# A planned one-core transformer block: quantization's powers of two copied by ScalarE, one buffer for MLP and quantization, other stage offsets

## The chip, the cores and the metric

The kernel runs on one core of a Trainium2 chip. Its engines are TensorE (PE, with weight loads listed apart as PEld), VectorE (DVE), ScalarE (ACT), GpSimd (POOL) and SyncE (SP), which here issues every DMA. Matrix products land in PSUM; all else lies in SBUF or in DRAM. Each engine takes its instructions in the order of its own list and waits for semaphores of the others.

The metric is the device time of one execution in microseconds, lower is better. Before the change it is 7728.81 us, the median of 3 runs (7723.64 to 7744.94).

## The reference

The input x has 16 sequences of 1024 tokens with 256 channels, all in fp32. Four residual steps follow each other:

```
x = x + attention(layernorm(x))     # 16 heads of 16, rotary, causal; Wqkv, Wproj
x = x + ffn(layernorm(x))
x = x + mixer(layernorm(x))         # returns y + silu(rmsnorm(y) @ w1.T) @ w2.T, y = z + mamba(rmsnorm(z))
x = x + ffn(layernorm(x))
```

The mamba part is an input product, a convolution over 4 tokens, a recurrence over 1024 steps for 512 channels with 16 states each, a gate and an output product. The step that the change is about is ffn. It takes blocks of 32 channels, divides each by its greatest absolute value over 7.5, rounds to the nearest value of a grid of six bits (ties to the lower one), multiplies back, and multiplies by a weight that was quantized in the same way:

```
scales = max(max|block| / 7.5, 1e-30)
q = nearest_on_grid(block / scales)     # grid: m/8 below 1, (1 + m/8) * 2^(e-1) above
out = (q * scales) @ (wq * ws).T + bias
```

## The kernel before

**Tiling and stages.** Each sequence is cut into two halves of 512 tokens, which gives 32 half sequences m; f = m % 2 tells the first half from the second. Work on one m is written as eight stages, each a function: `stage_a` (0: layernorm, transposes, queries and keys, rotary), `stage_m` (1: the scores' row maxima, for 8 pairs of heads), `stage_e` (2: values, scores again, exponentials, the product with the values), `stage_p` (3: output product, residual, and the first ffn), `stage_b` (4: mamba's inputs), `stage_s` (5: the recurrence, by VectorE's scan), `stage_o` (6: mamba's output product, rmsnorm), `stage_c` (7: the MLP, residual, and the second ffn). Stages p, b, o and c work on two tiles of 256 tokens, one after the other (i0 = 0 and 2). Stage c runs the MLP for each 128 tokens: for two groups of four hidden tiles a group of w1 products into a ps tile, a tanh by ScalarE and a multiply by VectorE into a hid tile, and then one group of 8 x w2 products from both hid tiles.

**Order.** Nothing is issued when a stage is called. `Graph` records each instruction (or group) as a node with its dependencies and an estimated cost (`add`, L971, and `_cost`, L1232). `prepare` (L1014) gives each node a due time: its place in its stage, counted by cost and spread over 32 units, one per half sequence, plus the stage's entry in OFFSETS. SP's nodes are due LEAD earlier, and nodes of other engines that read a ps tile URGENT earlier. `run` (L1058) then plays the program with the estimated costs: whenever an engine is free, it takes the ready node with the lowest due time whose tiles can be had. `emit` writes the instructions in that order, all from line 1167, so the profile tells groups apart by tile names and not by lines. The list of each engine is thus fixed before the kernel runs; what takes longer on the chip than in the plan makes an engine wait at the head of its list.

**Tiles.** A tile is taken from a ring of buffers when its first node is placed, and freed when its last user is done. Four rules bear on what follows:

- PSUM has six `ps` tiles of 128 x 512, shared by all stages, and one `av` and one `y`. `AT_ONCE` limits how many ps tiles a stage may hold. Within a stage ps tiles are taken in program order (`turn`, L1052 to L1056, tested in `lacks`, L1076); hid tiles likewise.
- The node that takes a ps tile also takes at once the tiles that its later users would take (L1036 to L1044), so that a product does not lie in PSUM with no place to go.
- Two nodes of different engines on the same PSUM tile are always ordered, reads too (L996).
- `y_s`, stage e's result, has two buffers, and one half sequence fills both (one for each 128 channels). Stage p's transposes of i0 = 0 and of i0 = 2 read both.

**The quantization** (`quantize`, L230 to L260) is called from `feed_forward` (L271), in stage p and in stage c, for both i0, and once for the weight: 129 times. VectorE finds the blocks' maxima; GpSimd multiplies the source by the inverse into r, which lies in the destination tile. VectorE masks the exponent bits into e (a ps tile), raises it to at least 1, and writes the exponent of the inverse into t (a hid tile). GpSimd multiplies r by t. ScalarE adds two constants in turn, which rounds: into odd (a ps tile) and into r. VectorE takes the smaller of the two into r, then takes off the constant and multiplies by e into t. GpSimd multiplies t by the scale into the destination. `feed_forward` then transposes the result into another hid tile (hT) and multiplies it by the weight.

The change touches `hid_tile` (L227), `quantize`, `feed_forward` (L276), `stage_c` (L801 to L825), and the numbers in BUFS, OFFSETS, LEAD, AT_ONCE and URGENT (L845 to L853).

Of the kernel before, what the change touches and what calls it, by code (L numbers as in the profile page):

```python
# [13 lines left out]
I32 = mybir.dt.int32  # L14
AF = mybir.ActivationFunctionType
ALU = mybir.AluOpType
# [3 lines left out]
P = 128  # L20
NT = T // P
KC = C // P
NH, DH = 16, 16
HT = T // 2
# [8 lines left out]
EXP_BITS = 0x7F800000  # L33
# [3 lines left out]
MAGIC = 1.5 * 2.0**21  # L37
# [3 lines left out]
def block_kernel(ctx: ExitStack, tc: tile.TileContext, a, out: bass.AP):  # L41
# [10 lines left out]
    g = Graph(raw, pools)  # L52
    nc = g

    def ps_tile():
        return g.tile([P, 512], "ps", 6, "psum", as_needed=True)
# [5 lines left out]
    def t2_tile(tag):  # L62

        return g.tile([P, 2, C], tag, BUFS[tag])
# [63 lines left out]
    vaug = wp.tile([P, BUFS["vaug"], VPAD], F32, tag="vaug", name="vaug")  # L128
# [8 lines left out]
    for n, tag in ((HT, "qt"), (HT, "kt"), (HT // 2, "dk"), (HT, "sh")):  # L137
        made = []
        for i in range(BUFS[tag]):
            t = wp.tile([P, n], F32R, tag=f"{tag}{i}", name=f"{tag}{i}")  # L140
# [6 lines left out]
    for i in range(BUFS["ovz"]):  # L147
        t = wp.tile([P, 512], F32, tag=f"ovz{i}", name=f"ovz{i}")
# [10 lines left out]
    def small(shape, tag, name):  # L159

        return g.tile(shape, f"{tag}_{name}", 2)
# [9 lines left out]
    def layernorm(x, dst, name):  # L171

        n = x.shape[1]
        st = small([P, n, 6], "st", name)
        mv = small([P, n, 2], "mv", name)
        with g.group():
            for i in range(n):
                nc.vector.bn_stats(out=st[:, i, :], in_=x[:, i, :])
                nc.vector.bn_aggr(out=mv[:, i, :], in_=st[:, i, :])
        rs = rstd_of(mv[:, :, 1], n, LN_EPS, name)  # L180
        shift = small([P, n], "sh", name)
        with g.group():
            nc.gpsimd.tensor_scalar_mul(shift, mv[:, :, 0], -1.0)
            nc.gpsimd.tensor_tensor(out=shift, in0=shift, in1=rs, op=ALU.mult)
        for i in range(n):
            nc.scalar.activation(
                dst[:, i, :], x[:, i, :], AF.Identity, bias=shift[:, i : i + 1], scale=rs[:, i : i + 1]
            )
        return mv[:, :, 1], rs
# [11 lines left out]
    def transpose_into(dst, src):  # L201

        ps = ps_tile().rearrange("p (c t) -> p c t", c=KC)
        with g.group():
            for c in range(KC):
                for i in range(2):
                    nc.tensor.transpose(ps[:, c, i * P : (i + 1) * P], src[:, i, c * P : (c + 1) * P], ident)
        nc.scalar.copy(dst, ps)

    def linear(dst, lhs, nk, w, biased=False):  # L210

        ps = ps_tile().rearrange("p (t c) -> p t c", c=C)
        with g.group():
            for i in range(2):
                for k in range(nk):
                    nc.tensor.matmul(
                        ps[:, i, :],
                        lhsT=lhs[k][:, i * P : (i + 1) * P],
                        rhs=w[:, k, :],
                        start=(k == 0),  # L220
                        stop=(k == nk - 1 and not biased),
                    )
                if biased:
                    nc.tensor.matmul(ps[:, i, :], lhsT=ones, rhs=bias, start=False, stop=True)
        nc.vector.tensor_tensor(out=dst, in0=dst, in1=ps, op=ALU.add)

    def hid_tile():  # L227
        return g.tile([P, HT], "hid", BUFS["hid"], as_needed=True)

    def quantize(src, dst, name):  # L230

        nb = 2 * C // 32
        shp = [P, nb, 32]
        srcb, dstb = (v.rearrange("p t (k e) -> p (t k) e", e=32) for v in (src, dst))
        amax = small([P, nb], "amax", name)
        inv = small([P, nb], "inv", name)
        most = ps_tile()[:, 0:nb]
        nc.vector.tensor_reduce(out=most, in_=srcb, axis=AX.X, op=ALU.max, apply_absolute_value=True)
        nc.vector.tensor_scalar(amax, most, 1.0 / 7.5, 1e-30, ALU.mult, ALU.max)
        nc.vector.reciprocal(out=inv, in_=amax)  # L240
        nc.scalar.mul(amax, amax, 0.5)
        t = hid_tile().rearrange("p (k e) -> p k e", e=32)
        r = dstb
        nc.gpsimd.tensor_tensor(
            out=r, in0=srcb, in1=inv.unsqueeze(2).to_broadcast(shp), op=ALU.mult
        )

        e = ps_tile().rearrange("p (k e) -> p k e", e=32)
        nc.vector.tensor_single_scalar(e.bitcast(I32), r.bitcast(I32), EXP_BITS, ALU.bitwise_and)
        nc.vector.tensor_single_scalar(e, e, 1.0, ALU.max)  # L250
        nc.vector.tensor_single_scalar(t.bitcast(I32), e.bitcast(I32), EXP_BITS, ALU.bitwise_xor)
        nc.gpsimd.tensor_tensor(out=r, in0=r, in1=t, op=ALU.mult)
        odd = ps_tile().rearrange("p (k e) -> p k e", e=32)
        for i, v in enumerate((odd, r)):
            nc.scalar.activation(v, r, AF.Identity, bias=magic[:, i : i + 1])
        nc.vector.scalar_tensor_tensor(r, r, -0.25, odd, ALU.add, ALU.min)
        nc.vector.scalar_tensor_tensor(t, r, -MAGIC, e, ALU.add, ALU.mult)
        nc.gpsimd.tensor_tensor(
            out=dstb, in0=t, in1=amax.unsqueeze(2).to_broadcast(shp), op=ALU.mult
        )  # L260
# [10 lines left out]
    def feed_forward(x, name, tag):  # L271

        h = t2_tile(tag)
        layernorm(x, h, f"f{name}")
        quantize(h, h, name)
        hT = hid_tile().rearrange("p (c t) -> p c t", c=KC)  # L276
        transpose_into(hT, h)
        linear(x, [hT[:, c] for c in range(KC)], KC, wd, biased=True)

# [515 lines left out]
    def stage_c(m):  # L795
        r2T = shifted.pop(m)
        for i0 in range(0, HNT, 2):
            x = t2_tile("c2")
            nc.sync.dma_start(out=x, in_=vds[m][i0 // 2])
            for i in range(2):  # L800
                hids = []  # L801
                t0 = (i0 + i) * P
                for k0 in range(0, NF, 4):
                    ps = ps_tile().rearrange("p (f t) -> p f t", f=4)
                    with g.group():
                        for k in range(4):
                            for c in range(KC):
                                nc.tensor.matmul(
                                    ps[:, k, :],
                                    lhsT=w1[:, c, (k0 + k) * P : (k0 + k + 1) * P],  # L810
                                    rhs=r2T[:, c, t0 : t0 + P],
                                    start=(c == 0),
                                    stop=(c == KC - 1),
                                )
                    psf = ps.rearrange("p f t -> p (f t)")
                    hidf = hid_tile()
                    hids.append(hidf)
                    nc.scalar.activation(hidf, psf, AF.Tanh, scale=0.5)
                    nc.vector.scalar_tensor_tensor(hidf, hidf, 1.0, psf, ALU.add, ALU.mult)
                ps = ps_tile()[:, 0:C]  # L820
                with g.group():
                    for k in range(NF):
                        nc.tensor.matmul(
                            ps,
                            lhsT=hids[k // 4][:, k % 4 * P : (k % 4 + 1) * P],  # L825
                            rhs=w2[:, k, :],
                            start=(k == 0),
                            stop=(k == NF - 1),
                        )
                nc.vector.tensor_tensor(out=x[:, i, :], in0=x[:, i, :], in1=ps, op=ALU.add)  # L830
            feed_forward(x, "b", "c2")
            nc.sync.dma_start(out=tokens(out, m, i0), in_=x)


    stages = (stage_a, stage_m, stage_e, stage_p, stage_b, stage_s, stage_o, stage_c)
    for m in range(2 * B):
        for s, stage in enumerate(stages):
            g.stage = s
            stage(m)
    g.prepare(OFFSETS, LEAD, URGENT)  # L840
    order = g.run()
# [1 line left out]


BUFS = {"kt": 4, "qt": 2, "dk": 3, "sh": 2, "ovz": 3, "ov": 2, "pt": 2, "hb": 4, "dx": 5, "a2": 1, "p2": 2, "y_s": 2, "b2": 2,  # L845
        "o2": 2, "c2": 2, "rot": 3, "hid": 2, "vaug": 8, "carry": 40}
W4 = 3

OFFSETS = (0.0, -0.3, -0.5, 0.2, 2.3, 4.1, 4.5, 5.3)
LEAD = 0.3  # L850

AT_ONCE = {("ps", 1): 4, ("ps", 2): 4, ("ps", 3): 3, ("ps", 5): 2}
URGENT = 0.1  # L853

# [87 lines left out]
class Graph:  # L944
# [113 lines left out]
    def run(self):  # L1058
# [17 lines left out]
        def lacks(n):  # L1076
            wanted = {}
            for t in n.reserve:
# [3 lines left out]
                wanted[s] = wanted.get(s, 0) + 1  # L1082
                full = s.held.get(t.line, 0) + wanted[s] > AT_ONCE.get((s.name, t.line), 99)
                if full or len(s.free) < wanted[s] or t.turn >= s.taken.get(t.line, 0) + wanted[s]:
# [285 lines left out]
```

## Time and profile before

| | |
|---|---|
| median of 3 runs | 7728.81 us |
| the profiled execution's own time | 7733.1 us |
| its span, first to last instruction | 7731.2 us |
| mean granted TensorE clock | 0.915 |
| DMA | 1460.35 MB, 62.2% of 16 engines' time |
| POOL idle before hb<-dx,bc | 953.1 us, of it 712.1 on PE's y and 169.1 on loads of dx |
| hid's MLP activations / copies of hT | 256 / 128 |

Where the stages of one half sequence lie in time is read from the starts of instructions that each stage alone has. For m = 16:

| stage | mark | us from the span's start |
|---|---|---|
| e | first and last write of y_s | 3631 to 3764 |
| p | last multiply of its two quantizations | 3790 and 3838 |
| b | first copy of rT, last store of dd | 3825 and 4006 |
| s | first multiply into hb, last gate yg | 4101 to 4373 |
| o | copies of r2T | 4396 and 4435 |
| c | last multiply of its two quantizations | 4524 and 4640 |

From stage s of m = 1 to that of m = 30 a half sequence takes 231 us. The last write of y_s (m = 31) is at 7283, 448 us before the end.

How to read the profile: a row gives line, engine, operation, output<-inputs with buffer numbers left out, shapes and count, then busy time and the mean of one in ns, then the engine's idle time before them and what ended most of it. Tiles that come from `t2_tile` carry the first letter of their tag (p in stage p, c in stage c), `ps` is any of the six PSUM tiles, w any of mamba's work tiles. A wait is named by what came last. Share of busy time is an average over 32 half sequences with a start and an end, so the windows view, which gives busy times for chosen stretches, stands beside the page.

### The profile page before, as it was taken

Reading aid. Unit: us, or ns where it says so; the run is one execution under the profiler, and the core shown is the slowest. Engines: PE = TensorE matmul, PEld = TensorE weight load, DVE = VectorE, ACT = ScalarE, POOL = GpSimd, SP = SyncE. Lnnn points to the kernel's source line nnn. Section 1 sums busy time; section 2 is a strip of 40 time slices with the busy share of each in tenths; the row PEclk is TensorE's granted clock in tenths of the full one; section 3 lists DMA queues with packets and bytes.
Section 4 is the critical chain, followed back from the end, with each engine's and each line's share of the span. In section 5 each row is a group of like instructions: output and inputs, shape, how many; then the busy total and the mean of one; then the engine's idle time right before and its main releaser. Section 6 shows DMA issues by size and latency. Waiting matters only on the chain. (4 is left out here: it accounts for less than half of the span.)

```text
span 7731.2 us, 133194 instructions
## 1 busy us (share of the span) xinstructions
PE 7019.5 (91%) x43012; PEld 4061.3 (53%) x43012; DVE 6308.6 (82%) x12351; ACT 5308.7 (69%) x11348; POOL 5016.3 (65%) x3948
## 2 busy tenths in 40 slices
PE   6999999999999999999999899999999999999866
PEld 4444555555455555555555555555555555555434
DVE  3488988888887878888888788888988888888885
ACT  3667677776767667676776767777676776867652
POOL 2366757665676666676666676666767766665784
PEclk8988999999999898998999899999999999999877
DMA  4566766765676566665656666566766666665562
GB/s 148 164 194 215 206 194 192 210 189 173 206 210 196 170 187 201 193 212 168 208 177 198 196 193 211 176 204 195 209 198 195 208 181 194 212 192 168 160 180 70
DMA packets 978300, 1460.35 MB, mean 189 GB/s; under 512 B 92720, under 2 KB 410800, under 8 KB 977600
## 3 DMA queue, kind: packets, MB, share of 16 engines
q1 hardware_dynamic: 977600, 1451.84, 62.2%
q8 instruction: 339, 5.55, 0.3%
q14 instruction: 361, 2.96, 0.1%
HBM read 1044.63 MB, written 371.20 MB: 183 GB/s over the span
## 5 line engine op out<-in xcount | busy, mean ns | idle before, releaser
L1167 POOL TENSOR_TENSOR hb<-dx,bc 128x1024 f32<-128x1024 f32 x1024 | 2411.8, 2365 | 953.1 <-PE y L1167 712.1
L1167 ACT ACTIVATE pt<-ps 128x512 f32<-128x512 f32 (+1 forms) x2560 | 1258.5, 557 | 499.0 <-PE ps L1167 478.9
L1167 ACT ACTIVATE ps<-dx,amat 128x512 f32<-128x512 f32 x2048 | 1402.2, 700 | 132.8 <-DVE hb L1167 95.2
L1167 DVE TENSOR_TENSOR_SCAN ps<-ps,h_carry,hb 128x512 f32<-128x512 f32 x768 | 963.4, 1278 | 121.8 <-ACT ps L1167 71.7
L1167 DVE TENSOR_TENSOR hb<-ps,ct 128x512 f32<-128x512 f32 x1536 | 1022.6, 680 | 8.1
L1167 DVE TENSOR_TENSOR_SCAN ps<-ps,hb 128x512 f32<-128x512 f32 x768 | 922.9, 1218 | 96.3 <-ACT ps L1167 40.9
L1167 PE MATMUL av<-pt,vaug 128*32 128x512 f32 (+3 forms) x6144 | 934.3, 536 | 36.3 <-ACT pt L1167 31.0
L1167 PE MATMUL ps<-qt,kt 64*128 64x512 f32 (+3 forms) x3072 | 799.0, 457 | 101.4 <-ACT pt L1167 20.8
L1167 POOL TENSOR_TENSOR hb<-hb,ct 128x1024 f32<-128x1024 f32 x256 | 604.9, 2363 | 340.4 <-ACT h_carry L1167 186.2
L1167 PE MATMUL y<-hb,ysel 128*32 128x512 f32 x4096 | 670.1, 655 | 84.4 <-POOL hb L1167 37.3
L1167 PEld LDWEIGHTS ps<-qt,kt 64*128 64x128 f32 x3072 | 349.5, 194 | 609.7 <-issue 148.8
L1167 PE MATMUL ps<-sh,ones 64*128 64x512 f32 (+3 forms) x3072 | 630.8, 370 | 5.4 <-DMA sh<-mr 5.2
L1167 POOL TENSOR_TENSOR w<-w,w 128x1024 f32<-128x1024 f32 x192 | 454.5, 2367 | 145.3 <-ACT w L1167 121.6
L1167 PE MATMUL ps<-r2T,w 128*128 128x128 f32 x4096 | 529.5, 285 | 15.5 <-ACT pt L1167 4.3
L1167 PEld LDWEIGHTS ps<-r2T,w 128*128 128x128 f32 x4096 | 492.1, 197 | 78.9 <-issue 22.3
L1167 PEld LDWEIGHTS ps<-kt,qt 64*128 64x128 f32 x3584 | 324.7, 205 | 388.0 <-issue 132.5
L1167 PE MATMUL ps<-kt,qt 64*128 64x128 f32 (+1 forms) x3584 | 460.4, 324 | 54.7 <-ACT pt L1167 14.1
L1167 PE MATMUL ps<-rT,w 128*128 128x512 f32 x1024 | 500.6, 616 | 9.2 <-ACT ovz L1167 1.9
L1167 ACT ACTIVATE ovz<-ps 128x384 f32<-128x384 f32 (+2 forms) x1024 | 366.2, 412 | 200.9 <-PE ps L1167 192.1
L1167 PE MATMUL ps<-dk,qt 64*128 64x256 f32 (+1 forms) x2560 | 405.4, 348 | 102.8 <-DVE mx L1167 24.7
L1167 PE MATMUL ps<-w,hid 128*128 128x256 f32 x2048 | 485.7, 392 | 9.8 <-ACT pt L1167 3.9
L1167 POOL TENSOR_TENSOR rot<-rot,rot 128x512 f32<-128x512 f32 (+1 forms) x256 | 361.0, 1410 | 199.3 <-DMA rot<-rot 82.4
(189 smaller groups left out, 14170.1 us busy)
## 6 DMA issues: line engine op xcount, KB each, us to landing
dx<-dd SPq DMA_DIRECT2D x2048, 256.0 KB
kt<-kd SPq DMA_DIRECT2D x384, 256.0 KB
kd<-rot SPq DMA_DIRECT2D x256, 256.0 KB
qd<-rot SPq DMA_DIRECT2D x256, 256.0 KB
qt<-qd SPq DMA_DIRECT2D x256, 256.0 KB
zxd<-w SPq DMA_DIRECT2D x128, 512.0 KB
dd<-w SPq DMA_DIRECT2D x128, 512.0 KB
dk<-ed SPq DMA_DIRECT2D x384, 128.0 KB
```

The source lines that it names most:

```text
L1167: getattr(getattr(self.nc, name), method)(*args, **kw)
```

## The change

The quantization's e becomes two tiles. The mask, the maximum and the exclusive-or work on `ep` in PSUM as before. A new ScalarE copy then puts it into e in SBUF. The smaller of the two roundings is written into odd, in PSUM, in place of r, and the last VectorE operation reads odd from PSUM and e from SBUF.

A hid buffer becomes twice as large ([P, 2, 512] for [P, 512]), and there is one of it in place of two. A quantization takes it whole (e and t), hT takes it whole and uses half, and an MLP takes it once for both groups.

The offsets of stages m, p, b, s, o and c change, LEAD, URGENT too, and two limits of AT_ONCE go (stage m's 4 and stage p's 3), so those stages may hold as many ps tiles as there are.

```diff
     def hid_tile():
-        return g.tile([P, HT], "hid", BUFS["hid"], as_needed=True)
+        return g.tile([P, 2, HT], "hid", BUFS["hid"], as_needed=True)
...
-        t = hid_tile().rearrange("p (k e) -> p k e", e=32)
+        both = hid_tile()
+        e, t = (both[:, i].rearrange("p (k e) -> p k e", e=32) for i in range(2))
...
-        e = ps_tile().rearrange("p (k e) -> p k e", e=32)
-        nc.vector.tensor_single_scalar(e.bitcast(I32), r.bitcast(I32), EXP_BITS, ALU.bitwise_and)
-        nc.vector.tensor_single_scalar(e, e, 1.0, ALU.max)
-        nc.vector.tensor_single_scalar(t.bitcast(I32), e.bitcast(I32), EXP_BITS, ALU.bitwise_xor)
+        ep = ps_tile().rearrange("p (k e) -> p k e", e=32)
+        nc.vector.tensor_single_scalar(ep.bitcast(I32), r.bitcast(I32), EXP_BITS, ALU.bitwise_and)
+        nc.vector.tensor_single_scalar(ep, ep, 1.0, ALU.max)
+        nc.vector.tensor_single_scalar(t.bitcast(I32), ep.bitcast(I32), EXP_BITS, ALU.bitwise_xor)
+        nc.scalar.copy(e, ep)
         nc.gpsimd.tensor_tensor(out=r, in0=r, in1=t, op=ALU.mult)
...
-        nc.vector.scalar_tensor_tensor(r, r, -0.25, odd, ALU.add, ALU.min)
-        nc.vector.scalar_tensor_tensor(t, r, -MAGIC, e, ALU.add, ALU.mult)
+        nc.vector.scalar_tensor_tensor(odd, r, -0.25, odd, ALU.add, ALU.min)
+        nc.vector.scalar_tensor_tensor(t, odd, -MAGIC, e, ALU.add, ALU.mult)
...
-        hT = hid_tile().rearrange("p (c t) -> p c t", c=KC)
+        hT = hid_tile()[:, 0].rearrange("p (c t) -> p c t", c=KC)
...
-                hids = []
+                hid = hid_tile()
...
-                    hidf = hid_tile()
-                    hids.append(hidf)
+                    hidf = hid[:, k0 // 4, :]
...
-                            lhsT=hids[k // 4][:, k % 4 * P : (k % 4 + 1) * P],
+                            lhsT=hid[:, k // 4, k % 4 * P : (k % 4 + 1) * P],
...
-        "o2": 2, "c2": 2, "rot": 3, "hid": 2, "vaug": 8, "carry": 40}
+        "o2": 2, "c2": 2, "rot": 3, "hid": 1, "vaug": 8, "carry": 40}
...
-OFFSETS = (0.0, -0.3, -0.5, 0.2, 2.3, 4.1, 4.5, 5.3)
-LEAD = 0.3
+OFFSETS = (0.0, -0.5, -0.5, 1.5, 2.1, 3.4, 3.8, 4.6)
+LEAD = 0.1
...
-AT_ONCE = {("ps", 1): 4, ("ps", 2): 4, ("ps", 3): 3, ("ps", 5): 2}
-URGENT = 0.1
+AT_ONCE = {("ps", 2): 4, ("ps", 5): 2}
+URGENT = 0.05
```

## The prediction

> **What bounds the kernel now.** I read the page first, for the engines' shares.
>
> ```profile
> PE 7019.5 (91%) x43012; PEld 4061.3 (53%) x43012; DVE 6308.6 (82%) x12351; ACT 5308.7 (69%) x11348; POOL 5016.3 (65%) x3948
> PEclk8988999999999898998999899999999999999877
> ```
>
> TensorE is the fullest engine, and no other is near enough to be the bound alone. Next, the windows view over the start, the body and the end; the columns are length, then busy time of PE, PEld, DVE, ACT and POOL, then granted clock, DMA share and GB/s.
>
> ```profile
> 0.00:193.00 193.00, 127.34 (x841) 79.02 (x841) 67.46 (x264) 67.86 (x158) 43.67 (x67) 0.86 0.47 149
> ...
> 1160.00:6900.00 5740.00, 5344.08 (x33237) 3112.72 (x33235) 4836.21 (x9510) 4085.12 (x8728) 3858.26 (x3026) 0.93 0.65 195
> ...
> 7300.00:7731.00 431.00, 276.17 (x1202) 164.90 (x1200) 319.27 (x437) 178.38 (x370) 280.43 (x199) 0.77 0.45 127
> ```
>
> In the body TensorE is busy 93%. It loses 66 us at the start and 155 us at the end, where only late stages of the last half sequences are left and its clock falls to 0.77. So there is little to win on TensorE, and much to lose: the body's 7% idle is what a better or worse order moves.
>
> Which order matters is seen in the rows of the tile y_s, here around the end of stage e of half sequence 16.
>
> ```profile
> L1167 PEld LDWEIGHTS ps<-ident,y_s x8: 139/140/145, 3766.1 to 3799.4; 128*128 128x128 f32 x8
> L1167 PE MATMUL ps<-ident,y_s x8: 272/273/330, 3766.1 to 3799.5; 128*128 128x128 f32 x8
> L1167 DVE TENSOR_TENSOR y_s<-av,rd x2: 291/292/292, 3764.0 to 3813.9; 128x128 f32<-128x128 f32 x2
> ```
>
> Stage e's last write is at 3764.0, stage p's first transpose at 3766.1, its last at 3799.5, and only then, at 3813.9, stage e of half sequence 17 writes. There are two y_s tiles, both needed by one half sequence, so e(m+1) waits for p(m)'s second transposes. These wait for p's whole first half, because ps tiles are taken in program order within a stage, and the first half's residual, layernorm, quantization and linear come before. Over all 32 half sequences the same rows give 39 us from e's last write to p's last transpose (26 to 58). A quantization of stage p thus lies on the loop m–e–p of the attention, although it looks like filler.
>
> **The change part by part.** The chain that ended last holds one quantization with nothing beside it (start, us, engine and output).
>
> ```profile
> 7713.52 0.70 DVE ps L1167
> ...
> 7714.25 0.71 DVE ps L1167
> ...
> 7714.98 0.70 DVE hid L1167
> ...
> 7715.81 1.27 POOL c L1167
> ...
> 7717.11 0.70 ACT ps L1167
> ...
> 7717.83 0.73 ACT c L1167
> ...
> 7718.59 0.70 DVE c L1167
> ...
> 7719.38 0.70 DVE hid L1167
> ```
>
> Two rows price the new operations: a ScalarE copy of that size from PSUM to SBUF, and a VectorE operation of that kind that writes PSUM.
>
> ```profile
> L1167 ACT COPY hid<-ps 128x512 f32<-128x512 f32 x128 | 75.7, 592 | 69.2 <-PE ps L1167 68.6
> ...
> L1167 DVE SCALAR_TENSOR_TENSOR ps<-w,convw,ps 128x512 f32<-128x512 f32 x384 | 276.7, 747 | 31.9 <-ACT ps L1167 30.0
> ```
>
> *The copy.* 129 quantizations (2 tiles x 2 places x 32, and the weight) x 0.592 = 76 us of ScalarE. It may start when the exclusive-or ends (7715.68) and lies beside the GpSimd multiply of 1.27 us, before the two roundings, so alone it costs nothing. Without that cover each costs 0.59. ScalarE's queue does grow 1.4%, and behind the copy wait exponentials that TensorE waits for. Between 0 and 76 I take +10, near the hidden end, since ScalarE is busy 69%.
>
> *The first rounding in PSUM.* 747 against 680 ns of the row it replaces: 129 x 0.067 = 9 us of VectorE, which is busy 82%. Bounds 0 and 9; I take +4. The last operation keeps one operand in each memory.
>
> *PSUM time.* Now e is held from the mask to the last operation, on average 11.8 us from these rows paired over 128 quantizations (5.9 in the chain above to the last operation's start). After, its ps tile is free after the copy: mask to exclusive-or is 3.6 us on average, about 5.1 with the copy. The odd tile is held 1.6 us longer. Net 5.1 us x 129 = 660 of 6 x 7731 = 46,390 tile-us, 1.4%. If PSUM were the only limit that is 110 us; if not, 0. TensorE's waits for readers of PSUM (DVE mx 346, ACT pt 301 and smaller ones) come to about 1000 us, and 1.4% of those is 14. I take -15, by that row.
>
> A rule speaks against the copy: the Trainium skill, "VectorE: DVE Perf Modes", section "Rules for kernel authors", advises to take the slower PSUM read or to copy first only where many operations follow. Here one operation follows the copy, and the rows show no cheaper read (681 ns now with e in PSUM, 683 for w<-ps,w). By that rule the sum would hold the copy's whole 76 us in place of 10; PSUM time is what the rule leaves out.
>
> *One hid buffer.* Today a quantization and an MLP can each hold one.
>
> ```profile
> L1167 ACT ACTIVATE hid<-ps x2: 597/597/597, 3372.7 to 3392.8; 128x512 f32<-128x512 f32 x2
> ...
> L1167 DVE TENSOR_SCALAR hid<-ps x1: 684/684/684, 3371.3 to 3371.3; 128x512 int32<-128x512 int32 x1
> ...
> L1167 POOL TENSOR_TENSOR p<-hid,amax_a x1: 1066/1066/1066, 3378.2 to 3378.2; 128x512 f32<-128x512 f32 x1
> L1167 ACT COPY hid<-ps x1: 585/585/585, 3381.6 to 3381.6; 128x512 f32<-128x512 f32 x1
> ```
>
> Stage p's quantization (3371.3 to 3379.3) and its transposed tile (from 3381.6) lie inside an MLP that runs from 3372.7 to its second half at 3392.8 and on. With one buffer they can't. Pairing such rows, an MLP holds hid 20.0 us from its first matmul to its last, a quantization 11.2 and a transposed tile 4.7; x 128 that is 4,600 us, 60% of one buffer. Existing overlaps come to 334 us in all, 160 of them in p's first halves, on the loop above (5 us per half sequence). Bounds 0, if MLPs move into gaps, and 334. Half of TensorE's work is outside the loop and can fill in, so I take +60, between a third and a half of 160.
>
> *Offsets.* A due time is m (spread over one half sequence) plus the stage's offset, and the lowest goes first. At 3764, by the marks of each stage, e is at due 16.5 while s is at 14.54 + 4.1 = 18.6 and c at 13.25 + 5.3 = 18.5. p(16), due 16.2 to 17.2, comes before both. With the new offsets p(16) is due 17.5 to 18.5, s is at 17.9 and c at 17.9. So p loses its rank and stands among s and c on PE, DVE, ACT and POOL, and e(m+1) waits behind it. The price is bounded by the same quantization in stage c, which has a low rank today: 12.9 us held against 9.4 in p, x1.37. On 39 us that is +14 per half sequence, 447 in all; nothing if s and c run short of input first, for then p is the lowest due again. s starts on average 63 us after b's last store, so this slack is short. I take +65, at the low end for that reason.
>
> Shorter lag of s, o and c (0.7 of 231 us) also empties the end sooner. The chain e, p, b, s, o, c of the last half sequence stays: s(31) starts 9 us after b(31)'s last store already, so only contention goes. Bounds 0 and -75 (half of the 155 us idle); I take -45.
>
> *LEAD, AT_ONCE, URGENT.* Loads are due 23 us ahead in place of 69. SP's issues in 256 KB loads for s are the ones at risk: POOL waited 196 us for dx. Loads are still listed when their buffer is free, as dx's five buffers decide, so 0, with +50 if a quarter more is lost. Stage m without a limit of 4 ps tiles could take all 6; its ov and ovz tiles hold it near 4: 0, between -20 and +40 by a fraction of the 346 us above.
>
> Sum: 10 + 4 - 15 + 60 + 65 - 45 = +79. Span 7731.2 + 79 = 7810; the profiled execution took 7733.1, 4 us above the median of 7728.8, which is less than the 23 us that I count as no change (0.3%). I predict 7810.
>
> **The rivals.** *Faster.* PSUM time and the shorter end decide, and p keeps its rank because s and c run out of input: -40 for PSUM (a third of its bound), -75 at the end, +10 for the copy, hid hidden: 7625 to 7690. For it: the slack of 63 us, and 155 us idle at the end. Against: hid at 60% on the loop. It decides where p's last transpose comes within 39 us after e's last write, as now.
>
> *No change.* TensorE at 93% takes up every delay with other stages' work, and gains and losses are below 23 us. For it: idle time in the body is 7% only. Against: five parts of different sign, none of which is bound to meet the others.
>
> *Much slower.* The loop waits as the bounds say: 447 + 160 for p's rank and hid, little filled in, less 45: 7900 to 8300. It would need p's last transpose 55 us or more after e's last write. Against: s waits in turn and gives p way.
>
> **How the numbers follow.** The forecast (up to some 2% slower) 0.47, faster 0.30, no change 0.10, much slower 0.13. Slower by over 0.3% is 0.47 + 0.13 = 0.60. The range starts at 7650, which leaves out the better half of the faster rival's span (about 0.10), and ends at 7940, which leaves out most of the much slower one (0.10). The likeliest case alone is 7755 to 7890.
>
> **What would show it.** 129 more ScalarE copies near 0.59 us; e's ps tile released before the GpSimd multiply ends; no overlap among hid's users; p's last transpose 45 to 55 us after e's last write; TensorE's body share near 92%; the end, after e's last write, shorter than now (448 us). The prediction is wrong if the loop's wait stays at 39 us, or if the body fills and the same work takes less time because PSUM was the limit.

## The result, and the profile after

The changed kernel takes 7767.13 us (median of 6 runs, 7752.54 to 7775.43); the kernel before takes 7732.88 in the same comparison. The ratio is 1.0035, with a 95% interval of 1.0019 to 1.0051: slower by some 30 us. Forecast were +79 us. The profiled execution has a span of 7763.7 us, 32.5 above that of before.

The page's engine line and clock line after:

```profile
PE 7011.6 (90%) x43012; PEld 4052.3 (52%) x43012; DVE 6313.4 (81%) x12351; ACT 5382.7 (69%) x11477; POOL 5015.3 (65%) x3948
PEclk8988999999999999998998999899998999998887
```

ScalarE has 129 instructions and 74 us more, as it should. TensorE is busy 8 us less and idle 40 us more. The windows view over the same three stretches (length, busy time of PE, PEld, DVE, ACT, POOL, clock, DMA share, GB/s):

```profile
0.00:193.00 193.00, 129.37 (x855) 80.35 (x857) 66.55 (x263) 68.95 (x159) 39.77 (x62) 0.87 0.48 149
...
1160.00:6900.00 5740.00, 5322.33 (x33095) 3092.46 (x33095) 4835.26 (x9472) 4135.85 (x8815) 3850.07 (x3015) 0.93 0.65 194
...
7300.00:7763.00 463.00, 298.63 (x1282) 175.84 (x1280) 331.47 (x456) 203.46 (x409) 298.66 (x210) 0.78 0.45 129
```

No stretch stands out. The body is as full as before, 92.7% against 93.1%. The rows of y_s around the end of stage e of half sequence 16 answer to those shown before:

```profile
L1168 PEld LDWEIGHTS ps<-ident,y_s x8: 137/140/141, 3759.1 to 3805.6; 128*128 128x128 f32 x8
L1168 PE MATMUL ps<-ident,y_s x8: 273/273/328, 3759.1 to 3805.7; 128*128 128x128 f32 x8
L1168 DVE TENSOR_TENSOR y_s<-av,rd x2: 291/292/292, 3758.0 to 3806.6; 128x128 f32<-128x128 f32 x2
```

Stage p's last transpose now starts 47.7 us after e's last write (35.5 there before), and the next half sequence's first write of y_s follows it at once. Over all 32 half sequences this time, called the wait below as in the prediction, is 50.7 us (39.2 before). Stage s starts on average 1 us after b's last store; by the same rows it was 53 us before, where the prediction says 63. The longer wait is what the prediction forecast. That s runs short of input is the condition under which it priced p's lost rank at nothing; the wait grew all the same.

Three groups price the new operations:

```profile
L1168 ACT COPY hid<-ps 128x512 f32<-128x512 f32 x257 | 151.7, 590 | 113.6 <-DVE hid L1168 56.1 <-PE ps L1168 55.7 <-DVE mr L1168 1.5
L1168 DVE SCALAR_TENSOR_TENSOR hid<-ps,hid 128x512 f32<-128x512 f32 x129 | 88.2, 684 | 4.8 <-POOL rstd_l L1168 0.5
...
L1168 DVE SCALAR_TENSOR_TENSOR ps<-p,ps 128x512 f32<-128x512 f32 x64 | 43.9, 687 | 27.2 <-ACT p L1168 25.0 <-ACT h_carry L1168 2.1
```

The copies (129 of the 257) take 0.59 us, the rounding into PSUM 687 ns for 680. From the same rows paired, ep lies in PSUM for 5.2 us (e lay there for 11.8) and odd for 5.2. The hid rows of one stretch show the one buffer:

```profile
L1168 PE MATMUL ps<-w,hid x27: 379/380/436, 3764.8 to 3783.5; 128*128 128x256 f32 x27
...
L1168 ACT ACTIVATE hid<-ps x2: 597/606/614, 3774.2 to 3777.6; 128x512 f32<-128x512 f32 x2
...
L1168 ACT COPY hid<-ps x2: 564/576/587, 3787.8 to 3800.9; 128x512 f32<-128x512 f32 x2
L1168 DVE TENSOR_SCALAR hid<-ps x1: 659/659/659, 3785.9 to 3785.9; 128x512 int32<-128x512 int32 x1
```

An MLP's last product starts at 3783.5, a quantization of stage p at 3785.9, its hT follows at 3800.9. No two users overlap anywhere in the run.

So each step of the change is in the trace, and the time moved by less than half of the forecast. To see where it moved, I cut the span at e's last write of y_s. Its row in the whole run, before and after:

```profile
L1167 DVE TENSOR_TENSOR y_s<-av,rd x256: 290/291/293, 95.8 to 7282.6; 128x128 f32<-128x128 f32 x128
```

```profile
L1168 DVE TENSOR_TENSOR y_s<-av,rd x256: 291/292/294, 94.8 to 7323.7; 128x128 f32<-128x128 f32 x128
```

Up to that write 41 us are lost; from there to the end, 448 us before and 440 after, 9 are won. Below, "main part" and "end" mean these two. Both come from one traced execution, and executions of one kernel differ: those of the kernel before beside the experiments took 7708 to 7765 us. A plan is the order that the planner writes for one set of numbers. Every ratio below is to the kernel before.

### The profile page after: what moved, and what is told of

It is laid out like the page before. It is cut to its first block, busy times and chain, and to the rows that moved or that the text cites. A ratio compares the mean times of both kernels' runs of the same rounds, so it can differ in the third digit from the quotient of the medians.

```text
span 7763.7 us, 133309 instructions
## 1 busy us (share of the span) xinstructions
PE 7011.6 (90%) x43012; PEld 4052.3 (52%) x43012; DVE 6313.4 (81%) x12351; ACT 5382.7 (69%) x11477; POOL 5015.3 (65%) x3948
## 5 line engine op out<-in xcount | busy, mean ns | idle before, releaser
L1168 DVE CUSTOM_DVE_ANT_0 unread<-ps,ovz 128x128 f32<-128x128 f32 (+3 forms) x768 | 338.8, 441 | 223.0 <-PE ps L1168 135.4
L1168 PE MATMUL ps<-rT,w 128*128 128x512 f32 x1024 | 505.8, 620 | 11.8 <-ACT pt L1168 4.5
L1168 PE MATMUL ps<-w,hid 128*128 128x256 f32 x2048 | 501.8, 401 | 14.1 <-DVE hid L1168 7.9
L1168 PE MATMUL ps<-kt,qt 64*128 64x128 f32 (+1 forms) x3584 | 440.8, 316 | 48.5 <-ACT pt L1168 16.5
```

Of the source, the lines that this page charges most:

```text
L1168: getattr(getattr(self.nc, name), method)(*args, **kw)
```

## Experiments

Theory 1, the prediction's: stage e waits for stage p, and p's rank and the one hid buffer set the length of that wait and so the time. Rival 2: other stages' work fills the wait, and 30 us is no more than what a new order does by chance. Rival 3: large effects of the parts cancel.

**The numbers alone** (`offs_only`): the kernel before with the new OFFSETS, LEAD, AT_ONCE and URGENT.

> The kernel before with the new OFFSETS, LEAD, AT_ONCE and URGENT alone; quantization and hid tiles as before. By the prediction (p's loss of rank sets the loop of stage e): +65 for the rank, -45 for the shorter end, about +20 us, with p's last transpose 44 to 52 us after e's last write (39 before, 51 with the whole change). If the wait of the loop is filled by other stages' work: time within 15 us of before although that wait grows as far. If the parts are large and cancel: more than 40 us slower, or more than 40 us faster.

Measured: 7772.55 us, 1.0042 (1.0030 to 1.0054). Wait 46.8 us, main part 7349, end 421. It fits the 20 us of theory 1 only roughly, and fits the scatter of rival 2 once the control below is known.

**The code alone** (`code_only`): the changed kernel with the old four numbers.

> The changed quantization and the one hid buffer with the old OFFSETS, LEAD, AT_ONCE and URGENT. By the prediction: copy +10, PSUM destination +4, PSUM time -15, hid +60, together about +59 us, and the loop's wait some 5 us longer than 39. If other work fills the waits: within 15 us of before. If PSUM time decides: 20 to 60 us faster.

Measured: 7837.73 us, 1.0127 (1.0112 to 1.0142). The loop's wait is 43.8 us, main part 7322, end 514. Slower than the whole change by 70 us: rival 3 holds here. By the cut above the loss shows at the end.

**The copy alone, in the old order** (`copy_same_order`):

```diff
         nc.vector.tensor_single_scalar(t.bitcast(I32), e.bitcast(I32), EXP_BITS, ALU.bitwise_xor)
+        g.nodes[-1].copied = e
...
                 getattr(getattr(self.nc, name), method)(*args, **kw)
+            if hasattr(n, "copied"):
+                self.nc.scalar.copy(n.copied.found(), n.copied.found())
```

> The kernel before, its order unchanged, with one more ScalarE instruction per quantization put into the finished list: it copies e onto itself in PSUM right after the exclusive-or. It measures the added ScalarE work alone, with no new plan and no PSUM time gained. By the prediction +10 us (hidden behind the GpSimd multiply); if ScalarE's place in the chain is exposed, up to 76 us.

Measured: 7774.61 us, 1.0055 (1.0041 to 1.0068), +42 us, where the bounds were 0 and 76. The row of the added copies:

```profile
L1170 ACT COPY ps<-ps 128x512 f32<-128x512 f32 x129 | 73.8, 572 | 119.7 <-DVE hid L1168 119.1
```

Besides their own 74 us ScalarE stands idle 119 us before them, at the head of its list, until the exclusive-or is done. In a list that was not planned with it, the copy is not hidden, and this run prices its place in the list with its work.

**The copy left out of the new order** (`after_no_copy`):

```diff
         nc.scalar.copy(e, ep)
+        g.nodes[-1].left_out = True
...
         for n in order:
+            if hasattr(n, "left_out"):
+                continue
```

> The changed kernel with its order as it is, but the new ScalarE copy is left out when the list is written, so e is not computed and the second tile of the quantization holds old values (one memset at the start gives it some). All else of the list stays. If the copy costs what the same-order run showed (+42 us), this is 35 to 45 us faster than the changed kernel, about 7725, at or below the kernel before. By the prediction's term (+10): about 7757. If the copy is hidden in this plan: 7767.

Measured: 7751.48 us, 1.0022 (1.0011 to 1.0033) against 1.0035 (1.0019 to 1.0051) with it. That is 10 us by the ratios and 16 by the medians, close to the term of +10, though the intervals overlap. In a list that was planned with it, most of the copy seems to be hidden.

**Two controls on the kernel before** (`ctl_c`: stage c's offset 5.31 for 5.30; `ctl_b`: stage b's 2.31 for 2.30).

> A control: the kernel before with stage c's offset 5.31 in place of 5.30, which changes nothing that any theory speaks of, but lets the planner write a new order. By the prediction's theory: within 5 us of before. If any new order scatters the time: 10 to 40 us off, up or down, and then a difference of 30 us between two plans needs no cause among the parts of the change.

> A second control: the kernel before with stage b's offset 2.31 in place of 2.30. If the first control's +62 us is what any new order does: again 20 to 80 us slower, or as far to the other side. If it was a peculiarity of that number: within 10 us of before.

Measured: 7798.51 us, 1.0080 (1.0067 to 1.0093), and 7766.81 us, 1.0038 (1.0025 to 1.0050). On the kernel before, a hundredth of one offset costs as much as the whole change, or more than twice as much. The page of `ctl_c` shows the same work:

```profile
PE 7066.1 (91%) x43012; PEld 4071.7 (52%) x43012; DVE 6315.8 (81%) x12351; ACT 5324.0 (68%) x11354; POOL 5016.7 (64%) x3948
```

The same 43,012 products keep TensorE busy 47 us longer, at a granted clock of 0.912 in place of 0.915, and it is idle 16 us more. Main part 7357, end 437: the end is untouched, the main part moves.

**Two controls on the changed kernel** (`ctl_after`: c's offset 4.61 for 4.60; `ctl_after_b`: b's 2.11 for 2.10).

> A control on the other side: the changed kernel with stage c's offset 4.61 in place of 4.60. If both kernels are picked from a scatter of plans: 20 to 80 us away from 7767, more likely slower. If the changed kernel's shorter lags make it robust: within 10 us of 7767.

> The changed kernel with stage b's offset 2.11: a third plan beside 7767 and 7775. If the new offsets make plans alike: 7755 to 7790. If plans scatter as with the old ones (7734 to 7798): anywhere from 7730 to 7820.

Measured: 7774.84 us, 1.0051 (1.0034 to 1.0067), and 7780.52 us, 1.0062 (1.0042 to 1.0083). Ends 445 and 433. These nudges move the changed kernel by 0.16% and 0.27%, less than those of the kernel before; the first is within the 10 us that its expectation called robust. Three plans of each do not show whether the new numbers make plans more alike.

**More plans of the two mixes** (`code_c`, `code_b`: the new code with the old numbers but c's offset 5.31, b's 2.31; `offs_c`: the old code with the new numbers but c's 4.61).

> The changed quantization and one hid buffer with the old numbers, but stage c's offset 5.31: a second plan of the same code and, to 0.01, the same offsets as the run that took 7838. If that code is dearer at the old offsets whatever the plan (the prediction: +59 against the old code's plans, which took 7734, 7767 and 7798, mean 7766): 7810 to 7850. If 7838 was scatter of plans: as likely 7740 to 7800.

> As the last, with stage b's offset 2.31 and c's 5.30: a third plan. Dearer code: 7810 to 7850. Scatter: 7740 to 7800.

> The old quantization and hid tiles with the new numbers, stage c's offset 4.61: a second plan beside the run that took 7773. If the new offsets are worth something in themselves (end shorter, less lost to TensorE's clock: 7773 and the changed kernel's 7767 and 7775 lie close together): 7755 to 7790. If they are neutral and plans scatter by 30 us to each side: anywhere from 7730 to 7820.

Measured: 7833.17 us, 1.0134 (1.0102 to 1.0167); 7825.21 us, 1.0120 (1.0093 to 1.0147); 7763.57 us, 1.0038 (1.0021 to 1.0055). The first two settle it: the new code at the old numbers is dearer in each of three plans. All four mixes, with main part and end from the trace of each run:

| code, numbers | ratios | main part, us | end, us |
|---|---|---|---|
| old, old | 1, 1.0038, 1.0080 | 7283, 7328, 7357 | 448, 439, 437 |
| new, old | 1.0127, 1.0120, 1.0134 | 7322, 7326, 7310 | 514, 499, 501 |
| old, new | 1.0042, 1.0038 | 7349, 7328 | 421, 419 |
| new, new | 1.0035, 1.0051, 1.0062 | 7324, 7329, 7366 | 440, 445, 433 |

The main part shows no dependence on the mix (means 7323, 7320, 7338, 7340, with up to 74 us between plans of one mix; the traced execution of `code_c` was 20 us below its kernel's median, that of `ctl_after_b` 20 above). Differences of some 20 us could not be seen. The end does: 442 on average, 505 with the new code, 420 with the new numbers, 439 with both. The end goes with how far s lies behind e. In the last four half sequences s ends 486 us after e in the kernel before, 544 to 568 with the new code at the old numbers, and 443 after the change. The end's window of `code_only`, and those of before and after, cut at e's last write:

```profile
7322.00:7836.00 514.00, 332.54 (x1427) 189.65 (x1425) 393.99 (x534) 213.49 (x431) 344.54 (x236) 0.76 0.46 130
```

```profile
7283.00:7731.00 448.00, 293.17 (x1304) 178.36 (x1296) 335.13 (x461) 186.76 (x384) 293.90 (x208) 0.78 0.45 129
```

```profile
7324.00:7763.00 439.00, 278.24 (x1172) 165.79 (x1172) 314.01 (x431) 182.58 (x377) 276.85 (x199) 0.77 0.44 126
```

`code_only` has 394 us of VectorE's work left after e, where before has 335 and after 314: s was behind, and 174 of its scans come after e's last write (142 before, 132 after), with TensorE 65% busy. So the cut tells where the loss shows: the main part of `code_only` has 32 scans fewer in it than that of the kernel before, and takes as long as other plans' main parts.

**Which part of the code** (`hid_only`: one buffer, old quantization, old numbers; `quant_only`: the changed quantization, e in a buffer of its own, two hid buffers, old numbers).

> The one hid buffer alone, old quantization (t takes one half of it), old numbers. The new code at the old numbers took 98 us more than before and its end, after e's last write, 499 to 514 us (437 to 448 with the old code). If the one buffer holds up stage c and, with it, s: end 480 to 515, time 7780 to 7840. If the quantization does it: end 435 to 455, time within the old code's scatter, 7734 to 7798.

> The changed quantization alone, with e in a buffer of its own (room from the row maxima's unread results, which go back into their ps tile), two hid buffers and the old numbers. If the copy and the rounding in PSUM do it: end 480 to 515, time 7780 to 7840. If the one buffer does it: end 435 to 455, time 7720 to 7798.

Measured: 7823.57 us, 1.0106 (1.0070 to 1.0142), end 467; 7798.04 us, 1.0089 (1.0064 to 1.0113), end 467. For the end neither expectation held. Each lengthens the end by 25 us over the mean of 442, of the 63 that both do together. With one plan of each, the ends are clear of the old code's 437 to 448, the times are not clear of its scatter. `quant_only` is not the quantization alone: to make room, results of the row maxima that nobody reads go to PSUM in place of SBUF, and VectorE is busy 6371 us (6309 in `code_only`).

**The loop's wait taken away** (`early_before`):

```diff
-                        elif f == 0 or j == 0:
-                            left = unread[:, 0 : n * P]
...
+        yTs = []
         for i0 in range(0, HNT, 2):
-            x = t2_tile("p2")
-            nc.sync.dma_start(out=x, in_=tokens(a["x"], m, i0))
-            yT = g.tile([P, KC, 2 * P], "yT", 1)
+            yT = g.tile([P, KC, 2 * P], "yT", 2)
+            yTs.append(yT)
...
             nc.scalar.copy(yT, ps)
+        for i0 in range(0, HNT, 2):
+            x = t2_tile("p2")
+            nc.sync.dma_start(out=x, in_=tokens(a["x"], m, i0))
+            yT = yTs[i0 // 2]
```

> The kernel before with the loop's wait taken away: stage p transposes both y_s tiles first, into two yT buffers, and then runs its two halves (room for the second yT: the row maxima's unread results go back into the ps tile they came from). e(m+1) should find y_s free some 5 us after e(m)'s last write in place of 39. If that wait sets the time, as the prediction has it: 150 to 500 us faster. If other work fills it: within the controls' scatter of 60 us, and TensorE's busy share stays near 92%.

Measured: 7795.88 us, 1.0076 (1.0060 to 1.0093). Its rows of y_s at the same place:

```profile
L1168 PEld LDWEIGHTS ps<-ident,y_s x8: 138/140/142, 3798.4 to 3799.1; 128*128 128x128 f32 x8
L1168 PE MATMUL ps<-ident,y_s x8: 272/273/328, 3798.4 to 3799.2; 128*128 128x128 f32 x8
L1168 DVE TENSOR_TENSOR y_s<-av,rd x3: 290/291/291, 3784.7 to 3849.7; 128x128 f32<-128x128 f32 x3
```

All eight transposes run within 1 us; the wait is 1.9 us on average in place of 39.2. Yet here e's next write comes at 3849.7, 52 us after its last, and the time is no better: main part 7313, end 475. What e waits for is its own product. The rows of av, the PSUM tile of that product, say so for `early_before` (here) and for the place in the kernel before that the prediction shows:

```profile
L1168 PE MATMUL av<-fold,yu x8: 275/275/323, 3848.3 to 3849.1; 128*128 128x64 f32 x8
```

```profile
L1167 PE MATMUL av<-fold,yu x9: 275/276/324, 3762.8 to 3813.0; 128*128 128x64 f32 x9
```

In both, e's next write (3849.7, 3813.9) follows the last step of its own first product within 1 us; in the kernel before p's last transpose had started at 3799.5, 14 us earlier. On average over the run that product is ready 33 us after e's last write, in the kernel before as in `early_before`, and the write comes at 44 and at 34. So of the 39 us only some 11 held e up, and in about half of the 31 cases nothing did; after the change the two times are 31 and 52 us, and in 27 cases e was held up.

The run has a side cost, from the first two lines of the edit: to make room, results of the row maxima that nobody reads go to PSUM in place of SBUF, and VectorE is busy 65 us more:

```profile
PE 7043.7 (90%) x43012; PEld 4042.0 (52%) x43012; DVE 6373.7 (82%) x12351; ACT 5327.2 (68%) x11362; POOL 5014.6 (64%) x3948
```

No run has this cost alone. TensorE's weight loads wait for the row maxima as long as before (241 us, 240 before), and even all 65 us taken off would leave the kernel about where it was, not 150 to 500 us faster. The wait that I had called the bound is gone and next to nothing is won. Theory 1 falls.

**p's rank** (`after_p02`: the changed kernel with p's offset 0.2).

> The changed kernel with p's offset back at 0.2. By the prediction p's lost rank costs 65 us: this is some 65 us faster than the changed kernel, about 7705, with the loop's wait back near 40 us. If other work fills that wait: the wait falls to 40 to 45 us and the time stays within the scatter of the changed kernel's plans, 7755 to 7795.

Measured: 7738.15 us, 1.0017 (1.0004 to 1.0030). The wait falls from 50.7 to 45.5 us, the end stays at 442, the main part is 7275. It is 14 us faster than the changed kernel by the ratios and 29 by the medians, less than half of the 65, and no more than a nudge of 0.01 does. Its traced execution was 19 us below its median, so the main part of 7275 flatters it.

**Only s, o and c earlier** (`short_new`: new code, old numbers but offsets 3.4, 3.8 and 4.6 for these three; `short_old`: the same for the old code; `short_new_c`: as the first, with 4.61).

> The new code with the old numbers, only s, o and c moved to 3.4, 3.8 and 4.6; p stays at 0.2 and the limits of AT_ONCE stay. If it is the earlier due times of s, o and c that keep s from falling behind: s's end stays some 440 to 510 us after e's in the body, the end falls to 420 to 445, time 7740 to 7790. If p's offset or the limits do it: end 490 to 515, time near 7830.

> The kernel before with only s, o and c moved to 3.4, 3.8 and 4.6. The new code with just that took 7714, end 418. If the earlier s, o and c are what is worth something, and the code nothing: 7690 to 7780, end 415 to 435, s's end some 500 us after e's all through the body. If the new code's PSUM time is what made 7714: 7740 to 7800.

> A control to the run of 7714: the same with c's offset 4.61. If 7714 is what these numbers give: 7700 to 7735. If it was a favourable plan among the scatter of 30 to 60 us: 7720 to 7780, with the end at 415 to 435 all the same and the difference in the time before e's last write.

Measured: 7713.56 us, 0.9974 (0.9962 to 0.9986); 7774.90 us, 1.0067 (1.0051 to 1.0082); 7780.35 us, 1.0064 (1.0046 to 1.0082). Ends 418, 437 and 408. With the new code these three offsets shorten the end by 87 to 97 us and need neither p's offset nor the limits. With the old code there is little to win (437). The time of `short_old` lies in both ranges of its expectation, and its end of 437 speaks for the second, that the new code made `short_new` fast; but the control has the same new code and is no faster. e's last write in `short_new` and in its control:

```profile
L1168 DVE TENSOR_TENSOR y_s<-av,rd x256: 290/291/293, 95.1 to 7297.9; 128x128 f32<-128x128 f32 x128
```

```profile
L1168 DVE TENSOR_TENSOR y_s<-av,rd x256: 291/292/294, 95.1 to 7384.1; 128x128 f32<-128x128 f32 x128
```

`short_new` beats both kernels, by 0.26% and by 0.6%. Its control shares its short end and loses 86 us in the main part, for a hundredth in stage c's offset. So it is a good plan, and its numbers are not shown to be better ones in general.

## Why the prediction was right in sign and wrong in size

**The step that failed** is the one that turned the loop's wait into time: "+65" for p's rank, and "+60" of the one hid buffer's 160, argued from e waiting for p. It begins with a misreading: "and only then, at 3813.9," puts e's write down to p's transposes, where e's own product was ready only at that moment. The wait grew as forecast (45 to 55 us were named, 50.7 measured), the new numbers alone lengthened it to 46.8, and hid's overlaps went. But 12 us more in each of 32 waits, some 370 us, moved the main part by 41, which is inside what plans of one mix scatter; and taking the whole wait away won nothing. Some 33 us of the wait pass while e makes its next product. That the rest is filled by the seven other stages, with TensorE 93% busy, is the likely reading; no run shows by which.

**The shorter end** was forecast at -45 and measured at -9. The mechanism was larger on both sides: the new numbers take 66 us off the new code's end, and the new code adds 63. I had given it to contention, where it went with the backlog of s behind e, and I had put the code's price on the loop instead of into that backlog.

**The code's total** of +59 was near: at the old numbers, +0.88% or 68 us over the mean of the old code's three plans. Its reason was not: no move of the main part is seen, and the end is 63 us longer. At the new numbers the same code adds 0.09%, 7 us (means 1.0049 and 1.0040): its price hangs on the offsets, which a sum of separate terms cannot hold.

**The copy**, +10: 10 to 16 us in the new order, with overlapping intervals; the 42 us in the old order lie within the bounds of 0 and 76. The Trainium skill, "VectorE: DVE Perf Modes", section "Rules for kernel authors", advises for a product in PSUM either to accept the slower read or to copy it out first if many operations follow. These runs agree for e, which VectorE wrote there: one operation follows, the copies cost 10 to 42 us, and no run shows a gain. **The rounding into PSUM**, +4: 7 to 9 ns each, 1 us. **PSUM time**, -15: the tile is freed after 5.2 us, forecast 5.1, but no run shows a gain; `quant_only` was slower than before, with copy, rounding and its 62 us of VectorE in it, so a small gain is not excluded.

**LEAD, URGENT and the limits**, 0: no run has them alone. POOL's wait for dx fell from 196 to 186 us.

**A term was missing**: the plan itself. Nudges of 0.01 put the kernel before 29 and 62 us slower (ratios 1.0038 and 1.0080), so it lies at the favourable edge of the three plans tried. Against their mean (1.0039) the changed kernel's three plans (mean 1.0049) are equal within the scatter. That is where the measured 0.35% belongs, as far as the runs go; a part that caused it cannot be named. That the sign came out as forecast was luck.

**The rivals.** "No change" had the mechanism that fits best, TensorE taking up delays with other stages' work, and was missed narrowly: 27 us by the ratio, where 23 were its bound. "Much slower" fell with theory 1. "Faster" rested on PSUM and the end: the first was not seen, the second was eaten by the code.

**Open:** why one plan's main part is 80 us longer than another's. TensorE's busy time for the same products differs by 84 us between the traced executions (6995 to 7079), its idle time by 80; from `short_new` to its control busy time grows by 41 and idle time by 36. No wait was found that explains it.

## What to carry to other kernels

Where a planner or any search writes the order, change a number that should not matter by a hundredth, in the kernel before and in the changed one, before giving a part of an edit credit or blame; here that alone moved the time by up to 0.9%, and both kernels sat at the favourable edge of the three plans tried of each. Cut the span where the stage that feeds the rest ends: main part and end told apart in a few runs what total times could not. And a wait on a loop costs only what no other work can fill: look first when the thing that waits is itself ready, and take the wait away once before pricing it.

## What the runs showed of the hardware that I had not expected

The granted clock differs between executions of one and the same kernel, and the time with it. In 80 executions of the kernel before, beside the experiments, the mean granted clock lay between 0.911 and 0.918 and the time between 7765 and 7708 us, the lower clock mostly with the longer time (correlation -0.80). Over the 20 traced executions, all of the same 43,012 products, TensorE was busy 6995 to 7079 us at clocks from 0.921 to 0.909. So one traced execution does not show whether an order has a lower clock. Some means do differ: `ctl_c` had 0.911 over 4 executions, none above 0.912, the kernel before 0.915, and the changed kernel 0.918 over 6, though it is the slower one. What sets the clock was not found.
